# Transfers over 125 and 127 partitions divided at partition 112, a bias added by VectorE, and V's small products spread over more steps of a graph layer

## The chip, the core and the metric

The kernel runs on one core of a Trainium2 chip. A core has five engines with queues of their own: TensorE (PE, with its weight loads shown as PEld), VectorE (DVE), ScalarE (ACT), GpSimd (POOL) and SyncE (SP). Transfers between memory and the on-chip buffers are issued from the queues of SP, ACT and POOL and run on the core's 16 DMA engines. The metric is the device time of one execution in microseconds, lower is better. Times of before: 1989.81, 2000.09 and 2001.78 us, median 2000.09.

## What is computed

One graph layer with a residual. 6250 nodes have 128 features each; 206250 edges are sorted by their target. The features are normalised and clipped at zero, each edge makes a message of its two ends, each node takes the maximum of its messages.

```python
h = jnp.maximum(_layernorm(x, axis=-1), 0.0)
x_i = h[dst]; x_j = h[src]
msg = jnp.concatenate([x_i, x_j - x_i], axis=-1) @ W.T + b
out = jax.ops.segment_max(msg, dst, num_segments=x.shape[0])
return x + jnp.where(jnp.isfinite(out), out, 0.0)
```

Since the target's part of a message is the same for all its edges, the kernel computes A (target part with the bias) and B (source part) for every node once. The result is x + A + the maximum of B over a node's sources.

## The kernel before

All engines' orders are written out by hand: each engine runs its instructions in the order in which the program emits them, and waits only for what it needs. There are four stages.

**Normalisation (to about 278 us).** The 6250 nodes are 50 blocks of L = 125 nodes, a node on each partition; ten blocks (GQ) are loaded as one tile `xs`, partitions 0 to 63 from SP's queue and 64 to 124 from ACT's. Three such tiles are loaded at the start and two more in the loop. `moments` computes mean and variance of ten blocks on VectorE. Then pairs of blocks go round: ACT scales (`xn`), TensorE transposes (`pt`), ACT clips (`hT`), TensorE makes `pm` (for each block a product of ones with `brow`, which holds the bias in its second half, and a product of `hT` with the weights), ACT copies the B half twice (`Bp`, in bf16, and `bo`) and the A half once (`ao`), VectorE and ACT make the two remainders of B in bf16. After ten blocks `bo` and `ao` are stored to the tables `Bt` (SP) and `At` (ACT). From the second ten blocks on, one piece of VectorE work on the edge lists (`pop`) stands behind each pair; a piece `shift` also has TensorE products `dup`.

**Edge lists (278 to 430 us).** VectorE finishes the edge lists; GpSimd begins to gather rows of `Bt` into `G` (each gather is one indirect transfer of 128 rows).

**Loop (430 to 1589 us).** 13 tiles of ten target lanes (49 columns each), 25 steps to a tile; each step handles two blocks. For the step that follows, TensorE makes `z` from V, ACT makes of it the one-hot matrix `oh` in two instructions (`far`, `oh`); for this step TensorE multiplies it with the three bf16 parts of B into `ps` (six products of 490 columns) and VectorE takes the maximum into `acc2`. V of the next tile is prepared beside that: `v_pieces` makes a list of pieces (comparisons and products on VectorE, then `mats`, one for each of the ten lanes, 13 small products on TensorE into `pv`, then ACT's copy to `Vb`), and every step starts with `per` of them, which is two. VectorE also runs through the gathered rows one by one (`stream_step`), and each eight rows go to the table M from SP.

**Tail (from 1589 us).** Five groups of the 49 columns (9, 9, 9, 11 and 11). For each, `xo` (rows of x) is loaded from SP's queue and `a` (rows of A) from ACT's, GpSimd gathers R from M column by column, TensorE transposes a column of `acc` and VectorE merges it with R; then VectorE closes the group with five operations and the result is stored from SP. In the first three groups all 128 lanes have nodes, in the last two the last lane has none. There, and for the first 127 lanes of the others, the transfers have 127 partitions; the 128th lane of the first three groups goes by a transfer of its own.

Of the kernel before, what the change touches and what calls it, by code (L numbers as in the profile page):

```python
# [30 lines left out]
F32 = mybir.dt.float32  # L31
# [8 lines left out]
P = 128  # L40
# [6 lines left out]
L = 125  # L47
LD = 49
# [13 lines left out]
def gnn_kernel(tc, x, src, dst, W, b, out):  # L62
    nc = tc.nc
    N, C = x.shape
# [7 lines left out]
    NBLK = W2 // P  # L72
# [5 lines left out]
    LASTD = N - (P - 1) * LD  # L78
    V = nc.vector
# [11 lines left out]
    with ExitStack() as ctx:  # L91
# [9 lines left out]
        with ExitStack() as body:  # L101
# [52 lines left out]
            with ExitStack() as pre:  # L154
# [13 lines left out]
                brow = pool.tile([1, 2 * C], F32, name="brow")  # L168
                V.memset(brow[:, :C], 0.0)
                nc.sync.dma_start(brow[:, C:], at(b, 0, [[C, 1], [1, C]]))  # L170
# [8 lines left out]
                def load_x(q0):  # L179
                    t = xg[q0] = xp.tile([L, GQ, C], F32, name="xs")  # L180
                    for e, (p0, p1) in zip((nc.sync, A_), ((0, 64), (64, L))):
                        e.dma_start(t[p0:p1], x_q[p0:p1, q0:q0 + GQ])  # L182
# [136 lines left out]
                for q0 in range(0, Q, GQ):  # L319
# [6 lines left out]
                    for i in range(0, GQ, 2):  # L326
# [10 lines left out]
                        for j in range(2):  # L337
                            T_.matmul(pm[:L, j], ones[:1, :L], brow, start=True, stop=False)  # L338
                            T_.matmul(pm[:L, j], hT[:, j, :L], wT, start=False, stop=True)  # L339
                        A_.copy(Bp[:L, 0, q:q + 2], pm[:L, :, :C])  # L340
                        A_.copy(bo[:, i:i + 2], pm[:L, :, :C])  # L341
                        A_.copy(ao[:, i:i + 2], pm[:L, :, C:])
# [6 lines left out]
                    for e, o, t in ((nc.sync, Bt_q, bo), (A_, At_q, ao)):  # L349
                        e.dma_start(o[:, q0:q0 + GQ], t)  # L350
# [73 lines left out]
            with ExitStack() as main:  # L424
# [12 lines left out]
                def v_pieces(t):  # L437
# [23 lines left out]
                    def mats(l):  # L461
                        for b_ in range(NBLK):
# [11 lines left out]
                    for l in range(nl):  # L474
                        ps.append(lambda l=l: mats(l))
# [91 lines left out]
                for d0, g in ((0, cut), (cut, cut), (2 * cut, LASTD - 2 * cut), (LASTD, 11), (LASTD + 11, LD - LASTD - 11)):  # L567
# [3 lines left out]
                    xo = fin.tile([P, GF, C], F32, name="xo")[:np_, :g]  # L571
                    for e, t, s in ((nc.sync, xo, x), (A_, a, At)):
                        e.dma_start(t[:P - 1], at(s, d0 * C, [[LD * C, P - 1], [1, g * C]]))
                        if np_ == P:
                            e.dma_start(t[P - 1:], at(s, ((P - 1) * LD + d0) * C, [[LD * C, 1], [1, g * C]]))
# [16 lines left out]
                    nc.sync.dma_start(at(out, d0 * C, [[LD * C, P - 1], [1, g * C]]), xo[:P - 1])  # L592
                    if np_ == P:
                        A_.dma_start(at(out, ((P - 1) * LD + d0) * C, [[LD * C, 1], [1, g * C]]), xo[P - 1:])
# [62 lines left out]
```

## Time and profile before

| What | Value |
|---|---|
| Median of 3 runs | 2000.09 us |
| The profiled execution, own time | 1993.71 us |
| Its span on the core | 1991.9 us |
| TensorE busy | 1151.7 us, 58% |
| VectorE busy | 954.9 us, 48% |
| ScalarE busy | 767.5 us, 39% |
| GpSimd busy | 724.3 us, 36% |
| Mean granted TensorE clock | 0.764 of 2.4 GHz |
| Moved by DMA | 105.38 MB, mean 53 GB/s |

The busy shares are averages over four stages that are limited by different things, so they are read stage by stage: a table of stretches gives, for each, the busy time of every engine, the granted clock and the DMA share. Within a stage the timeline shows instructions in order of time, with the idle time ahead of each and what ended it. A queue's rows (SPq, ACTq) are issues of transfers; their length is the time that the queue was held by the issue, not the transfer's.

### The profile page before, as it was taken

How to read it: one execution, taken by the hardware profiler on the slowest of the kernel's cores; microseconds unless marked ns; L12 is line 12 of the kernel's file. 1: busy time of each engine (PE TensorE's matmuls, PEld its weight loads, DVE VectorE, ACT ScalarE, POOL GpSimd, SP SyncE). 2: the span in 40 equal slices, each digit the busy share in tenths (PEclk: the TensorE clock that was granted, in tenths of full speed). 3: DMA queues.
4: the chain of work that ended last, by engine and by line, in shares of the span. 5: the costliest groups of instructions: out<-in, count | busy, mean ns of one | idle time of the engine just before them, and what ended most of it. 6: DMA issues, size and time to landing. Idle time of an engine off the chain costs nothing.

```text
span 1991.9 us, 14462 instructions
## 1 busy us (share of the span) xinstructions
PE 1151.7 (58%) x4855; PEld 519.8 (26%) x4862; DVE 954.9 (48%) x1913; ACT 767.5 (39%) x958; POOL 724.3 (36%) x678
## 2 busy tenths in 40 slices
PE   0556677058686878587878778787879800000000
PEld 0222233034242433242433334242424300000000
DVE  4122149865657474947474756656566610110020
ACT  0223212224789454445455554646456800000000
POOL 6000018605646564446455546456551021202000
PEclk9999999557889787787778788768688955555555
DMA  3111011002222222122222222222221011101000
GB/s 79 34 42 32 26 30 36 24 7 65 73 64 81 68 83 66 56 67 70 65 77 70 66 74 75 74 64 71 65 78 52 26 44 36 37 25 38 27 26 23
DMA packets 53775, 105.38 MB, mean 53 GB/s; under 512 B 12342, under 2 KB 31221, under 8 KB 53695
## 3 DMA queue, kind: packets, MB, share of 16 engines
q0 software_dynamic: 21392, 45.22, 8.6%
q1 hardware_dynamic: 21931, 51.21, 7.0%
q10 hardware_dynamic: 10372, 7.98, 1.3%
q8 instruction: 39, 0.64, 0.1%
q14 instruction: 41, 0.34, 0.1%
HBM read 54.91 MB, written 49.45 MB: 52 GB/s over the span
## 4 chain that ended last, share of the span: by engine, by line
PE 35%; another core or an unknown queue 17%; DVE 15%; ACT 12%; issue 9%; POOL 4%; DMA 3%; ACTq 3%; DVEq 0%; POOLq 0%
PE ps L511 14%; PE pv L464 7%; PE z L488 6%; ACT oh L492 5%; ACT far L491 4%; POOL G L88 4%; DVE acc L516 3%; PE pm L339 3%; PE pm L338 3%; DVE G L148 3%; ACTq L182 3%; DMA a<-At 2%; ACT dump L528 1%; DVE OHQ L454 1%
## 5 line engine op out<-in xcount | busy, mean ns | idle before, releaser
L511 PE MATMUL ps<-oh,Bp 126*128 126x490 bf16 (+1 forms) x1950 | 563.9, 427 | 218.0 <-ACT oh L492 88.8
L88 POOL DMA_INDIRECT G<-Bt,ridx x480 | 485.4, 1011 | 416.2 <-DVE G L148 220.3
L516 DVE TENSOR_TENSOR acc<-acc,ps 128x490 f32<-128x490 f32 (+1 forms) x624 | 406.7, 654 | 439.2 <-PE ps L511 267.9
L491 ACT ACTIVATE far<-z 126x980 bf16<-126x980 f32 (+1 forms) x325 | 314.9, 969 | 467.4 <-PE z L488 230.8
L511 PEld LDWEIGHTS <-Bp 126*128 126x128 bf16 x1950 | 193.0, 106 | 558.8 <-issue 364.5
L492 ACT ACTIVATE oh<-far 126x980 bf16<-126x980 bf16 (+1 forms) x325 | 327.5, 1008 | 10.6
L88 POOL DMA_INDIRECT G<-Bt,swin x128 | 161.5, 1262 | 393.9 <-DMA Bt<-bo 247.2
L488 PE MATMUL z<-Vb,Sel 51*126 51x490 bf16 (+1 forms) x650 | 233.1, 444 | 0.7 <-ACT Vb L476 0.7
L464 PE MATMUL pv<-OHD,OHQ 128*50 128x49 bf16 x1664 | 170.1, 276 | 82.2 <-issue 61.3
L148 DVE SCALAR_TENSOR_TENSOR G<-G,slim 128x128 f32<-128x128 f32 x607 | 209.8, 346 | 0.0
L581 PE MATMUL pf<-ident,acc 128*128 128x128 f32 x49 | 20.1, 469 | 300.2 <-DVE R L582 295.7
L464 PEld LDWEIGHTS <-OHQ 128*50 128x50 bf16 x1664 | 161.0, 190 | 121.6 <-issue 95.5
L88 POOL DMA_INDIRECT R<-M,last_e x49 | 47.5, 969 | 257.6 <-DVE R L582 155.5
L488 PEld LDWEIGHTS <-Sel 51*126 51x126 bf16 x650 | 68.1, 147 | 128.7 <-issue 124.0
L344 DVE TENSOR_TENSOR r<-bo,Bp 125x256 f32<-125x256 f32 x25 | 10.6, 426 | 170.2 <-ACT bo L341 170.2
L581 PEld LDWEIGHTS pf<-ident,acc 128*128 128x128 f32 x49 | 8.9, 206 | 311.2 <-DVE R L582 304.5
L588 DVE TENSOR_TENSOR R<-R,a 128x1152 f32<-128x1152 f32 (+1 forms) x5 | 7.3, 1465 | 170.9 <-DMA a<-At 170.8
L297 PE MATMUL dup<-eq,identb 128*128 128x512 bf16 (+1 forms) x245 | 60.8, 371 | 34.6 <-DVE eq L294 27.2
L590 DVE TENSOR_TENSOR R<-R,xo 128x1152 f32<-128x1152 f32 (+1 forms) x5 | 7.3, 1465 | 119.9 <-DMA xo<-in_x 119.9
L333 PE MATMUL pt<-ident,xn 125*128 125x125 f32 x50 | 19.5, 452 | 75.4 <-ACT xn L331 75.4
L339 PE MATMUL pm<-wT,hT 128*125 128x256 f32 x100 | 60.8, 710 | 0.0
L338 PE MATMUL pm<-brow,ones 1*125 1x256 f32 x100 | 60.6, 706 | 0.0
(145 smaller groups left out, 689.8 us busy)
## 6 DMA issues: line engine op xcount, KB each, us to landing
M<-G SPq DMA_DIRECT2D x76, 512.0 KB
G<-Bt,ridx POOLq DMA_INDIRECT x480
Bt<-bo SPq DMA_DIRECT2D x5, 625.0 KB
At<-ao ACTq DMA_DIRECT2D x5, 625.0 KB
G<-Bt,swin POOLq DMA_INDIRECT x128
a<-At ACTq DMA_DIRECT2D x3, 571.5 KB
xo<-in_x SPq DMA_DIRECT2D x3, 571.5 KB
out_x<-xo SPq DMA_DIRECT2D x3, 571.5 KB
```

The source lines that it names most:

```text
L88: G_.indirect_dma_start(out=o, out_offset=None, in_=table, in_offset=bass.IndirectOffsetOnAxis(ap=idx, axis=0))
L148: V.scalar_tensor_tensor(G[:, j], state["prev"], slim[:, k:k + 1], G[:, j], op0=ALU.min, op1=ALU.max)
L182: e.dma_start(t[p0:p1], x_q[p0:p1, q0:q0 + GQ])
L297: T_.matmul(dup[:, c0:c1], identb, e[:, c0:c1], start=s == 1, stop=s == SH)
L338: T_.matmul(pm[:L, j], ones[:1, :L], brow, start=True, stop=False)
L339: T_.matmul(pm[:L, j], hT[:, j, :L], wT, start=False, stop=True)
L464: T_.matmul(st["v"][:, l * LD:(l + 1) * LD], st["q"][:, :Q, c], st["d"][:, :, c], start=b_ == 0, stop=b_ == NBLK - 1)
L488: T_.matmul(z[:, j, :n], Sel[:, i + j], Vb[t % 2][:, :n], start=True, stop=True)
L491: A_.activation(far[:, :, :n], z[:, :, :n], AF.Abs)
L492: A_.activation(oh[:, :, :n], far[:, :, :n], AF.Relu, scale=-1.0, bias=1.0)
L511: T_.matmul(ps[:, :n], Bp[:, e, i + j], oh[:, j, :n], start=e == 0, stop=e == 2)
L516: V.tensor_tensor(a, a, ps[:, :n], ALU.max)
```

## The change

It has three parts.

- Transfers are divided by partition. Over 125 nodes (loads of `xs`, stores of `bo` and `ao`): partitions 0 to 111 and 112 to 124. For `xs` the first part goes from SP, the second from ACT; for a store both parts go from the same queue. In the tail, the three groups with all lanes use one transfer over 128 partitions for each of x, A and the result, and the last two groups use partitions 0 to 111 and 112 to 126; the second part of their store goes from ACT.
- The product of ones with `brow` is gone. The bias is loaded into all 125 partitions (`b_sb`), and VectorE writes `ao` as the sum of the A half of `pm` and the bias, in place of ACT's copy.
- In `v_pieces` a lane's 13 small products are two pieces, of 7 and 6. As every step takes two pieces, they stand in ten steps of a tile and not in five, and the copy to `Vb` stands five steps later.

```diff
+    SPLIT = ((0, L // 16 * 16), (L // 16 * 16, L))
...
-                brow = pool.tile([1, 2 * C], F32, name="brow")
-                V.memset(brow[:, :C], 0.0)
-                nc.sync.dma_start(brow[:, C:], at(b, 0, [[C, 1], [1, C]]))
+                b_sb = pool.tile([L, 1, C], F32, name="b_sb")
+                A_.dma_start(b_sb[:, 0], at(b, 0, [[0, L], [1, C]]))
...
-                    for e, (p0, p1) in zip((nc.sync, A_), ((0, 64), (64, L))):
+                    for e, (p0, p1) in zip((nc.sync, A_), SPLIT):
...
-                            T_.matmul(pm[:L, j], ones[:1, :L], brow, start=True, stop=False)
-                            T_.matmul(pm[:L, j], hT[:, j, :L], wT, start=False, stop=True)
+                            T_.matmul(pm[:L, j], hT[:, j, :L], wT, start=True, stop=True)
...
-                        A_.copy(ao[:, i:i + 2], pm[:L, :, C:])
+                        V.tensor_add(ao[:, i:i + 2], pm[:L, :, C:], b_sb.to_broadcast([L, 2, C]))
...
-                        e.dma_start(o[:, q0:q0 + GQ], t)
+                        for p0, p1 in SPLIT:
+                            e.dma_start(o[p0:p1, q0:q0 + GQ], t[p0:p1])
...
-                    def mats(l):
-                        for b_ in range(NBLK):
+                    def mats(l, r):
+                        for b_ in r:
...
-                        ps.append(lambda l=l: mats(l))
+                        for r in (range(0, 7), range(7, NBLK)):
+                            ps.append(lambda l=l, r=r: mats(l, r))
...
+                    lanes = ((0, P),) if np_ == P else ((0, P - 16), (P - 16, P - 1))
                     for e, t, s in ((nc.sync, xo, x), (A_, a, At)):
-                        e.dma_start(t[:P - 1], at(s, d0 * C, [[LD * C, P - 1], [1, g * C]]))
-                        if np_ == P:
-                            e.dma_start(t[P - 1:], at(s, ((P - 1) * LD + d0) * C, [[LD * C, 1], [1, g * C]]))
+                        for p0, p1 in lanes:
+                            e.dma_start(t[p0:p1], at(s, (p0 * LD + d0) * C, [[LD * C, p1 - p0], [1, g * C]]))
...
-                    nc.sync.dma_start(at(out, d0 * C, [[LD * C, P - 1], [1, g * C]]), xo[:P - 1])
-                    if np_ == P:
-                        A_.dma_start(at(out, ((P - 1) * LD + d0) * C, [[LD * C, 1], [1, g * C]]), xo[P - 1:])
+                    for e, (p0, p1) in zip((nc.sync, A_), lanes):
+                        e.dma_start(at(out, (p0 * LD + d0) * C, [[LD * C, p1 - p0], [1, g * C]]), xo[p0:p1])
```

On TensorE, a pair of blocks in the normalisation stage stood like this before (transposes of the pair, then for each block the bias product and the product with the weights):

```order
L333 MATMUL pt<-ident,xn 128x125 x2
L338 MATMUL pm<-brow,ones 125x256
L339 MATMUL pm<-wT,hT 125x256
L338 MATMUL pm<-brow,ones 125x256
L339 MATMUL pm<-wT,hT 125x256
```

and now like this; the next pair's transposes follow at once:

```order
L333 MATMUL pt<-ident,xn 128x125 x2
L338 MATMUL pm<-wT,hT 125x256 x2
```

On ACT, the head of the program before and now, up to the first scaled block. The loads of `xs` have 13 partitions in place of 61, and the load of the bias stands ahead of them:

```order
L165 DMA lasts_i<-in_dst 1x375x1
L182 DMA xs<-in_x 61x10x128 x3
L251 ACT_TABLE_LOAD
L251 COPY wT<-pm 128x256
L314 ACT_TABLE_LOAD
L314 ACTIVATE rstd<-mv,eps 125x10 x2
```

```order
L166 DMA lasts_i<-in_dst 1x375x1
L170 DMA b_sb<-in_L_gnn_b 125x128
L182 DMA xs<-in_x 13x10x128 x3
L251 ACT_TABLE_LOAD
L251 COPY wT<-pm 128x256
L314 ACT_TABLE_LOAD
L314 ACTIVATE rstd<-mv,eps 125x10 x2
```

On SP, the last two groups of the tail, from the third group's store on. A group's load of x stands behind the store of the group ahead of it in both orders; before, one transfer of 127 partitions each:

```order
L592 DMA out_x<-xo 127x1152
L573 DMA xo<-in_x 127x1408
L592 DMA out_x<-xo 127x1408
L573 DMA xo<-in_x 127x1408
L592 DMA out_x<-xo 127x1408
```

and now two loads and, for SP, the larger part of each store:

```order
L594 DMA out_x<-xo 128x1152
L576 DMA xo<-in_x 112x1408
L576 DMA xo<-in_x 15x1408
L594 DMA out_x<-xo 112x1408
L576 DMA xo<-in_x 112x1408
L576 DMA xo<-in_x 15x1408
L594 DMA out_x<-xo 112x1408
```

## Rows read from the trace of the kernel before

**Rows 1.** Stretches: length, busy us (instructions) by engine, granted clock, DMA share, GB/s.

```profile
278.20:430.00 151.80, 66.21 (x381) 36.98 (x386) 124.07 (x130) 22.84 (x14) 80.79 (x48) 0.70 0.11 30
430.00:1589.50 1159.50, 918.79 (x4144) 410.56 (x4143) 712.41 (x1510) 678.31 (x763) 566.14 (x560) 0.81 0.21 67
1589.50:1991.90 402.40, 20.07 (x49) 8.89 (x49) 50.23 (x76) 0.00 (x0) 47.49 (x49) 0.50 0.09 32
```

**Rows 2.** Stretches again: stores of 125 partitions, a 127-partition transfer, a write of M.

```profile
282.00:290.00 8.00, 7.38 (x30) 3.07 (x29) 7.17 (x8) 0.00 (x0) 0.00 (x0) 1.00 0.35 103
1870.00:1895.00 25.00, 0.00 (x0) 0.00 (x0) 0.00 (x0) 0.00 (x0) 0.00 (x0) 0.50 0.06 27
908.20:909.60 1.40, 1.40 (x5) 0.51 (x4) 0.44 (x1) 1.37 (x2) 0.00 (x0) 0.50 0.93 374
```

**Rows 3.** Timeline of the tail: start, length, engine, line, operation, [idle before <-releaser].

```profile
1605.86 0.97 DVE L587 TENSOR_SCALAR none<-R 128x1152 f32<-128x1152 f32 x1
...
1637.26 1.36 DVE L588 TENSOR_TENSOR R<-R,a 128x1152 f32<-128x1152 f32 x1 [30.42 <-DMA a<-At]
...
1642.76 0.33 DVE L582 SCALAR_TENSOR_TENSOR R<-R,limp,pf 128x128 f32<-128x128 f32 x1
...
1643.22 19.25 SPq L573 DMA_DIRECT2D xo<-in_x  x1
...
1644.39 0.94 POOL L88 DMA_INDIRECT R<-M,last_e  x1 [0.30 <-issue]
...
1649.24 0.76 DVE L587 TENSOR_SCALAR none<-R 128x1152 f32<-128x1152 f32 x1
...
1960.38 0.23 SPq L592 DMA_DIRECT2D out_x<-xo  x1
```

**Rows 4.** Timeline of one pair's products in the normalisation; then the page's group r.

```profile
106.20 1.21 PE L338 MATMUL pm<-brow,ones 1*125 1x256 f32 x2
106.31 0.38 ACT L335 ACTIVATE hT<-pt 128x250 f32<-128x250 f32 x1 [0.56 <-PE pt L333]
...
107.34 1.22 PE L339 MATMUL pm<-wT,hT 128*125 128x256 f32 x2
...
L344 DVE TENSOR_TENSOR r<-bo,Bp 125x256 f32<-125x256 f32 x25 | 10.6, 426 | 170.2 <-ACT bo L341 170.2
```

**Rows 5.** Timeline of the start; then, from the waits, ACT's waits on its issues.

```profile
2.31 40.90 ACTq L182 DMA_DIRECT2D xs<-in_x  x3
...
34.58 0.75 DVE L312 BATCH_NORM_AGGREGATE mv<-stats 125x2 f32<-125x6 f32 x10
...
49.83 0.48 ACT L331 ACTIVATE xn<-xs,nmr,rstd 125x128 f32<-125x128 f32 x1
...
ACT xn L331 <- issue: 12.7, 2, 6.8
```

**Rows 6.** Timeline of the loop, ninth tile, steps 10 to 20: ACT's far, TensorE's products.

```profile
1212.74 0.99 ACT L491 ACTIVATE far<-z 126x980 bf16<-126x980 f32 x1 [0.92 <-PE z L488]
...
1217.13 2.67 PE L464 MATMUL pv<-OHD,OHQ 128*50 128x49 bf16 x26 [1.81 <-DVE OHQ L454]
...
1220.74 2.63 PE L511 MATMUL ps<-oh,Bp 126*128 126x490 bf16 x6
...
1221.30 0.99 ACT L491 ACTIVATE far<-z 126x980 bf16<-126x980 f32 x1 [6.53 <-PE z L488]
...
1226.45 1.42 PE L511 MATMUL ps<-oh,Bp 126*128 126x490 bf16 x6
...
1245.44 0.99 ACT L491 ACTIVATE far<-z 126x980 bf16<-126x980 f32 x1 [6.47 <-PE z L488]
...
1257.09 0.99 ACT L491 ACTIVATE far<-z 126x980 bf16<-126x980 f32 x1
```

## The prediction

> **What bounds the kernel now.** I read the stage table first (busy time by stretch). It cuts the span in a loop of 1159.5 us in which TensorE is busy for 918.79 us at a mean granted clock of 0.81 of 2.4 GHz, a stretch before it in which VectorE is busy for 124.07 of 151.8 us, and a tail of 402.4 us in which no engine is busy for more than 50.23 us [rows 1]. The 278.2 us ahead of these are the normalisation stage. So the tail is bound by something that is no engine. The DMA rates say what: while a transfer of 127 partitions is alone in flight, the core's 16 DMA engines are 0.06 busy, one sixteenth, and move 27 GB/s; while two stores of 125 partitions run, the share is 0.35 and the rate 103 GB/s; during one write of M, 128 partitions, it is 0.93 and 374 GB/s [rows 2]. The partition count sets how many engines work. The tail's timeline shows the price: VectorE waits 30.42 us for a group's rows of A and x, works 5.50 us (1637.26 to 1642.76), and the cycle starts again [rows 3]. In the normalisation stage ACT, TensorE and VectorE hand one pair of blocks round in series [rows 4], and ACT's own issue of x loads stops it [rows 5]. In the loop a pair's step takes about 2.3 us without V products and up to 8.6 us with them [rows 6].
>
> **The tail.** Edit: three groups load, and store, 128 partitions in one transfer; the last two go as 112 and 15. By rows 2 that takes 571.5 KB from about 22 us to under 2. What is left is VectorE's own chain, in the order it has today. Nine columns of R take 6.48 us (1642.76 to 1649.24), 0.72 each. The closing operations of such a group take 0.77 for the first and 5.50 for the other four, 6.27, or 0.70 a column. For 49 columns: 49 x 1.42 = 69.6 us. The first group is paced by its gathers: its closing begins at 1605.86, 16.4 us after the tail's start instead of 6.5, so 9.9 more. The last store: today 31.5 us pass from its issue at 1960.38 to the end of the span; 698.5 KB at 27 GB/s are 25.9 of them, so 5.6 are fixed, and at 374 GB/s it is 1.9 + 5.6 = 7.5. Sum 87 us against 402.4: **-315 us**. Three things are taken as hidden. GpSimd's gathers cost 0.95 + 0.30 each, 61 us for 49, under the 69.6. The next group's x load still stands behind this group's store on SP (1643.22, just after the copy of 1637.26 to 1642.76 ended), so it has 6.48 + 0.77 us and two of the four closing operations, some 10 us, as cover; store and load together are 1.14 MB, 3.1 us at 374 GB/s, plus the fixed 5.6, near 9. If that cover is missed by 5 us in each of five groups, the gain is 290. Past the best case, with the first group's 9.9 also gone, it is 325. In the last two groups ACT's load of A now stands behind ACT's 15-partition store, thus behind VectorE's closing too; it has the same cover. One issue more or less a group on SP and ACT is off the path, since neither queue has anything else to do there. A part of 15 partitions is in no row. Between one engine (82.5 KB at 27 GB/s, 3.1 us) and many (under 0.3) the last store differs by 3 us at most, the other parts lie under the cover; I take many, as the 0.35 for 125 shows that it need not be one.
>
> [...]
>
> **Normalisation, TensorE.** Each of 50 blocks loses its bias product. In a pair the first one starts at 106.20 and holds the product with hT until 107.34, though hT is ready at 106.31 + 0.38 = 106.69: 0.6 us. The second stands in the chain with its whole 1.14 us (the spacing of 106.20 and 107.34). So 1.74 x 25 = **-43.5 us**. The pair is one serial loop, so nothing else steps in its place. VectorE's new addition writes 125x256; its nearest row is r of the same shape, 426 ns, before which VectorE idles 170.2 us in 25 pairs, 6.8 each, for ACT's bo. The addition can run while ACT makes Bp and bo, so I cost it at nothing; were it to stand ahead of r it would cost 25 x 0.43 = 11 us. ACT's dropped copy of ao ran while ACT waited for r anyway: nothing.
>
> **Normalisation, loads.** ACT issues three x loads of 61 partitions and is held until 2.31 + 40.90 = 43.21 us, though the statistics it needs next stand at 34.58 + 0.75 = 35.33; its first xn comes at 49.83 [rows 5]. With 13 partitions it has a fifth of the rows, on many engines. I take 9 us: 7.9 from those two times and a little for the work that then also falls ahead of 35.33 (bounds 5 to 13). Twice later ACT's xn waits on its own issue, 12.7 us in all [rows 5]; I take 12 of it (bounds 6 to 12.7). The bias row, loaded to 125 partitions, is 62.5 KB on ACT's queue, which no longer blocks. SP's loads grow from 64 to 112 partitions, but SP has nothing else to do. The store of Bt in front of the first gathers gets faster as well; that I cost at nothing, since the stretch behind it is VectorE's (124.07 us busy of 151.8) and the gathers run beside that. Two issues per store in place of one: SP idles, and ACT pays five issues more, which I leave to the bounds. Dropping brow's memset and load saves nothing, as VectorE's next work there waits for a load of dst. **-21 us**.
>
> **The loop.** V's products for the next tile stand in steps 10 to 14 of 25, 26 to a step; they will stand in steps 10 to 19, 13 to a step. The work is the same; what can change is how they mix. From step 10 at 1212.74, five steps with products take 32.70 us, the next five without take 11.65, 44.35 together [rows 6]. 26 products take 2.67 us, so 13 take 1.33. Added to a plain step of 2.33 that is 3.66, ten steps 36.6: -7.7 a tile, x 12 tiles with products = -93. That needs TensorE at its upper level, where six products of ps take 1.42. At its lower level they take 2.63, 1.21 more, so 4.87 a step and 48.7 for ten: +4.4 a tile, +52. Which one? After 26 products the ps products behind them run at 2.63 (1220.74), yet one step on at 1.42 (1226.45) [rows 6], so the level recovers between groups even today, and smaller groups leave a larger share to the big products. I take eight steps at the upper level and two at the lower: 39.0, -5.3 a tile, **-64 us**. Nothing waits for the later end: V is copied at step 20, and step 24 is the first to read it.
>
> **Sum.** 315 + 43.5 + 21 + 64 = 443.5. The profiled execution took 1993.7 us (span 1991.9 and 1.8 around it): **1550 us**. The median of the three runs is 2000.1, 6 above it, which is within their spread.
>
> **Rivals.** (1) The loop loses: the spread products hold TensorE at 1.2 GHz through ten steps instead of five, +52 instead of -64. For it: 2.63 at 1220.74. Time 1993.7 - 379.5 + 52 = 1666. (2) The loop gains all: 1993.7 - 379.5 - 93 = 1521, and lower where the waits behind the products shrink with them; for it speaks that five steps cost 32.70 us and their products only 5 x 2.67 = 13.4. (3) The split brings nothing, because two parts share what one had; only the product and the loop count: 1993.7 - 43.5 - 64 = 1886. Against it stand the rates of rows 2. [...] (4) Slower: a step's price comes from changing between small and large products, not from their number. The first product step takes 1212.74 to 1221.30, 8.56 us; if all ten cost that, a tile loses 85.6 - 44.35 = 41.2, twelve 495, against 379.5 gained: 2109. It decides from 379.5 / 120 = 3.2 us above today's mean of 4.44, that is 7.6 us a step; the mean of the five product steps today, 6.54, is below that, and gives 1866.
>
> **How the numbers follow.** The forecast, with the loop between -105 and -20, 0.55; rival 1, with anything from there to +80, 0.22; rival 2, 0.18; rival 3, 0.03; rival 4, 0.02. The tail's bounds add -10 to +25, the small terms -4 to +20. The forecast's own range is 1500 to 1620. To leave out no more than 2 in 10, I take rival 2 down to 1455 and rival 1 up to 1670. A measurement of this kernel tells about 1% from no change. Faster by over 1% holds everything but rival 4: 0.97; slower 0.02, and 0.01 for sums that cancel.
>
> **What would show it.** Right: a tail of 80 to 110 us with VectorE busy for half or more of it and no wait for A or x over 3 us; a pair of blocks 1.7 us shorter than now; the first xn before 43 us; a tile of the loop in 80 to 90 us. Wrong: waits for xo of 5 us and more in the tail (the cover misses), ps products at 2.63 through steps 10 to 19, or a tile above 93 us.

## The result and the profile after

The changed kernel took 1595.55 us (median of 4 runs, 1586.28 to 1602.89), the kernel before 1994.95 us beside it (4 runs, 1969.96 to 2001.78). The ratio is 0.806 with a 95% interval of 0.795 to 0.816; it leaves out the two runs of before that are more than 1.5% slower than its fastest, and so lies above the quotient of the medians, 0.80. The profiled execution took 1599.15 us, its span 1597.4. Forecast were 1550 us, 1455 to 1670.

The stage table of the changed kernel (as [rows 1]: stretch, length, busy us and instructions of PE, PEld, DVE, ACT and POOL, granted clock, DMA share, GB/s); its four stages are the normalisation from its first xn on, the edge list, the loop and the tail:

```profile
42.20:218.30 176.10, 81.44 (x180) 42.28 (x183) 53.77 (x163) 56.15 (x153) 3.48 (x1) 0.90 0.15 37
218.30:370.00 151.70, 66.24 (x381) 36.85 (x385) 123.84 (x131) 22.59 (x13) 76.57 (x48) 0.68 0.11 30
370.00:1492.30 1122.30, 902.08 (x4139) 409.97 (x4138) 710.39 (x1507) 679.46 (x763) 565.27 (x560) 0.84 0.22 69
1492.30:1597.40 105.10, 21.04 (x57) 9.25 (x54) 51.70 (x79) 0.00 (x0) 49.68 (x49) 0.51 0.41 123
```

Against [rows 1] the normalisation ends at 218.3 in place of 278.2 (-59.9), the edge list is unchanged (151.7 against 151.8), the loop has 1122.3 in place of 1159.5 (-37.2) and the tail 105.1 in place of 402.4 (-297.3). Together these are 394.5 us, the difference of the two profiled executions.

Stretches of the changed kernel's tail in which the 128-partition loads run, against the 127-partition ones of [rows 2], and one with the last group's loads and a store in flight:

```profile
1497.50:1499.00 1.50, 0.00 (x0) 0.00 (x0) 0.00 (x0) 0.00 (x0) 1.02 (x2) 0.50 1.01 412
1577.00:1578.00 1.00, 0.49 (x1) 0.20 (x1) 0.41 (x2) 0.00 (x0) 0.00 (x0) 0.50 0.98 220
```

By these shares all 16 engines work: 0.06 and 27 GB/s became 1.01 and 412. In the second row the engines are as busy, 0.98, but move 220 GB/s.

VectorE's timeline in the tail (start, length, engine, line, operation, [idle before <- releaser]), with one of TensorE's transposes and SP's last store:

```profile
1508.57 0.76 DVE L588 TENSOR_SCALAR none<-R 128x1152 f32<-128x1152 f32 x1
...
1521.92 0.76 DVE L588 TENSOR_SCALAR none<-R 128x1152 f32<-128x1152 f32 x1
...
1534.83 0.76 DVE L588 TENSOR_SCALAR none<-R 128x1152 f32<-128x1152 f32 x1
...
1545.69 0.35 DVE L583 SCALAR_TENSOR_TENSOR R<-R,limp,pf 128x128 f32<-128x128 f32 x1 [1.43 <-remote]
...
1548.90 0.49 PE L582 MATMUL pf<-ident,acc 128*128 128x128 f32 x1 [2.32 <-issue]
...
1551.29 0.35 DVE L583 SCALAR_TENSOR_TENSOR R<-R,limp,pf 128x128 f32<-128x128 f32 x1 [2.44 <-remote]
...
1562.17 0.89 DVE L588 TENSOR_SCALAR none<-R 127x1408 f32<-127x1408 f32 x1
...
1578.03 0.89 DVE L588 TENSOR_SCALAR none<-R 127x1408 f32<-127x1408 f32 x1
1581.43 1.63 DVE L589 TENSOR_TENSOR R<-R,a 127x1408 f32<-127x1408 f32 x1 [2.50 <-DMA a<-At]
...
1588.15 0.33 SPq L594 DMA_DIRECT2D out_x<-xo  x1
```

The wait of 30.42 us in [rows 3] is gone; one of 2.50 is left. From one closing to the next pass 13.35, 12.91, 27.34 and 15.86 us. The third of these holds the columns of group 4, which come every 2.8 us behind a wait for "remote", a releaser that the profile can't name.

One pair of the normalisation, as [rows 4], on ACT and VectorE, with TensorE's products for the next:

```profile
51.86 0.37 ACT L339 CAST Bp<-pm 125x256 bf16<-125x256 f32 x1 [2.16 <-PE pm L338]
52.13 0.38 ACT L340 COPY bo<-pm 125x256 f32<-125x256 f32 x1
52.54 0.42 DVE L341 TENSOR_TENSOR ao<-pm,b_sb 125x256 f32<-125x256 f32 x1 [4.10 <-ACT bo L340]
52.88 0.42 DVE L343 TENSOR_TENSOR r<-bo,Bp 125x256 f32<-125x256 f32 x1
...
55.08 0.38 ACT L335 ACTIVATE hT<-pt 128x250 f32<-128x250 f32 x1 [0.56 <-PE pt L333]
...
55.52 2.07 PE L338 MATMUL pm<-wT,hT 128*125 128x256 f32 x4 [0.47 <-ACT hT L335]
57.62 0.37 ACT L339 CAST Bp<-pm 125x256 bf16<-125x256 f32 x1 [2.16 <-PE pm L338]
```

A pair takes 57.62 - 51.86 = 5.76 us. But the addition stands ahead of r after all: it starts at 52.54, just after ACT has read the same PSUM tile for bo (52.13 + 0.38 = 52.51), and r starts 0.34 us behind it.

### The profile page after: what moved, and what is told of

It is laid out like the page before. It is cut to its first block, busy times and chain, and to the rows that moved or that the text cites. A ratio compares the mean times of both kernels' runs of the same rounds, so it can differ in the third digit from the quotient of the medians.

```text
span 1597.4 us, 14322 instructions
## 1 busy us (share of the span) xinstructions
PE 1073.3 (67%) x4756; PEld 499.2 (31%) x4762; DVE 963.3 (60%) x1937; ACT 761.7 (48%) x933; POOL 721.4 (45%) x678
## 4 chain that ended last, share of the span: by engine, by line
PE 40%; DVE 14%; ACT 12%; issue 12%; POOL 5%; another core or an unknown queue 4%; DMA 1%; ACTq 0%; DVEq 0%; SPq 0%; POOLq 0%
PE ps L512 20%; PE pv L464 10%; PE z L489 8%; ACT far L492 5%; ACT oh L493 5%; POOL G L89 5%; DVE acc L517 3%; DVE G L149 3%; DVE OHQ L454 1%; ACT dump L529 1%; DVE OHD L454 1%; DVE OHD L459 1%; DVE big L549 1%; PE pf L582 1%
## 5 line engine op out<-in xcount | busy, mean ns | idle before, releaser
L512 PE MATMUL ps<-oh,Bp 126*128 126x490 bf16 (+1 forms) x1950 | 545.1, 417 | 199.3 <-ACT oh L493 98.7
L464 PE MATMUL pv<-OHD,OHQ 128*50 128x49 bf16 x1664 | 183.3, 277 | 79.4 <-issue 64.4
L489 PE MATMUL z<-Vb,Sel 51*126 51x490 bf16 (+1 forms) x650 | 227.4, 434 | 2.8 <-issue 2.0
L464 PEld LDWEIGHTS <-OHQ 128*50 128x50 bf16 x1664 | 165.2, 189 | 142.9 <-issue 122.9
L341 DVE TENSOR_TENSOR ao<-pm,b_sb 125x256 f32<-125x256 f32 x25 | 10.6, 425 | 109.7 <-ACT bo L340 104.3
L454 DVE TENSOR_TENSOR OHD<-TD,IQ 128x910 bf16<-128x910 bf16 (+1 forms) x91 | 52.9, 619 | 12.8 <-PE pv L464 12.7
L338 PE MATMUL pm<-wT,hT 128*125 128x256 f32 x100 | 51.4, 667 | 11.8 <-ACT hT L335 11.8
L459 DVE TENSOR_TENSOR OHD<-OHD,TV 128x910 bf16<-128x910 bf16 (+1 forms) x91 | 52.8, 619 | 0.0
L454 DVE TENSOR_TENSOR OHQ<-TQ,IQ 128x1300 bf16<-128x1300 bf16 (+1 forms) x65 | 50.9, 818 | 0.0
L297 PEld LDWEIGHTS <-identb 128*128 128x128 bf16 x252 | 26.1, 104 | 73.5 <-issue 54.2
```

The costliest lines, as they stand in the source:

```text
L297: T_.matmul(dup[:, c0:c1], identb, e[:, c0:c1], start=s == 1, stop=s == SH)
L338: T_.matmul(pm[:L, j], hT[:, j, :L], wT, start=True, stop=True)
L454: V.tensor_tensor(st[key][:, a:b_, :m], mid_bcast(src_[:, s], b_ - a), IQ[:, a + off:b_ + off, :m], ALU.is_equal)
L459: V.tensor_tensor(o, o, mid_bcast(TV[:, s], b_ - a), ALU.mult)
L464: T_.matmul(st["v"][:, l * LD:(l + 1) * LD], st["q"][:, :Q, c], st["d"][:, :, c], start=b_ == 0, stop=b_ == NBLK - 1)
L489: T_.matmul(z[:, j, :n], Sel[:, i + j], Vb[t % 2][:, :n], start=True, stop=True)
```

## The experiments

Where a stage is named, its length is from the stage table of that run; a table of the loop's steps stands behind the experiments on the loop.

**1. The tail alone.** The kernel before with this part of the change:

```
-  e.dma_start(t[:P - 1], ...)            (127 partitions, then 1)
+  lanes = ((0, P),) if np_ == P else ((0, P - 16), (P - 16, P - 1))
+  for p0, p1 in lanes: e.dma_start(t[p0:p1], ...)
```

> The kernel before with the tail's part of the change alone (128-partition transfers in three groups, 112 and 15 partitions in two). Theory: the tail is its own stage and depends on nothing else of the change: it falls from 402.4 to about 105 us as in the changed kernel, the rest stays, so about 1995 - 297 = 1698 us. Rival: part of the tail's gain comes with the other parts (M's last writes and the gathers arriving earlier in the shorter loop): then the tail stays above 120 us and the time above 1712 us.

Measured: 1684.12 us (1676.30 to 1686.22) beside 1999.51, ratio 0.8425 (0.8385 to 0.8464).

```profile
430.10:1580.60 1150.50, 928.67 (x4140) 412.84 (x4140) 710.55 (x1507) 678.48 (x763) 563.40 (x560) 0.80 0.21 67
1580.60:1682.80 102.20, 20.99 (x56) 9.24 (x54) 52.13 (x79) 0.00 (x0) 49.61 (x49) 0.52 0.43 126
```

The tail falls by 300.2 us with nothing else changed, so its gain is its own. The whole is 14 us below the theory's figure: 3 of that in the tail, 9 in the loop, which was not touched (1150.5 against 1159.5): the loop differs from run to run, by up to 30 us in the changed kernel (1102.9 to 1132.7, listed under 7).

**2. V's products back in five steps,** in the changed kernel:

```
-  for r in (range(0, 7), range(7, NBLK)):
+  for r in (range(0, NBLK),):
```

> The changed kernel with V's products back in five steps of 26. Theory: the loop's shortening (1159.5 to 1122.3 us) comes from the spread products alone, so the loop returns to 1150 to 1165 us and the whole to about 1595 + 37 = 1632 us. Rival: the late signals in the loop move with whatever comes ahead of it, and the spread itself is worth little: then the loop stays below 1140 us and the whole below 1615 us. What the prediction said (64 us) would give 1659 us.

Measured: 1634.14 us (1627.27 to 1641.28), ratio 0.8173 (0.8133 to 0.8213).

```profile
369.30:1532.60 1163.30, 928.53 (x4138) 412.41 (x4138) 710.57 (x1507) 678.34 (x763) 568.45 (x560) 0.79 0.21 66
```

The loop is 41.0 us longer than the changed kernel's 1122.3, and 35 longer than the mean of experiments 3 and 4 (1124.7 and 1132.7), which ran on the same chip with the changed loop. The theory holds in size: the spread products are worth 35 to 41 us, not 64.

**3. The normalisation's transfers as before** (x in 64 and 61 partitions, stores of 125 in one):

```
-  zip((nc.sync, A_), SPLIT)
+  zip((nc.sync, A_), ((0, 64), (64, L)))
-  for p0, p1 in SPLIT: e.dma_start(o[p0:p1, ...], t[p0:p1])
+  e.dma_start(o[:, ...], t)
```

> The changed kernel with the normalisation's transfers as before: x loads of 64 and 61 partitions, stores of 125 in one. Theory, from the two traces: the first xn returns from 42.15 to about 50 us (+8), ACT's issue waits at the later loads return (+5), and the last store of Bt, ahead of the first gathers, takes about 13 us again in place of 5 (+8 if something waits for it): the stretch ahead of the loop grows from 370 by 13 to 21 us, the whole to about 1595 + 17 = 1612 us. Rival: the loads' faster landing is hidden but for ACT's own issue, +5 us or less, 1600 us.

Measured: 1613.83 us (1609.04 to 1619.33), ratio 0.809 (0.805 to 0.813). The loop begins at 387.8 in place of 370.0: +17.8, inside the theory's 13 to 21; the first xn stands at 52.30 in place of 42.15.

**4. The bias as a product again,** with ACT's copy of ao:

```
+  T_.matmul(pm[:L, j], ones[:1, :L], brow, start=True, stop=False)
-  V.tensor_add(ao[:, i:i + 2], pm[:L, :, C:], b_sb.to_broadcast([L, 2, C]))
+  A_.copy(ao[:, i:i + 2], pm[:L, :, C:])
```

> The changed kernel with the bias again as a product into pm, and ACT's copy of ao. Theory: a pair of blocks returns from 5.75 to 7.46 us, 25 x 1.71 = 43 us, and the whole comes to 1638 us. Rival: the two products would overlap with the faster loads' slack, and VectorE's addition, which stands in front of r for 0.34 us a pair, has eaten part of the gain: then it costs under 30 us and the whole is under 1625 us.

Measured: 1629.45 us (1624.12 to 1643.35), ratio 0.814 (0.811 to 0.817). The loop begins at 411.8, +41.8 us, and two successive Bp of ACT stand at 47.65 and 55.10, 7.45 apart; from the pair's hT to its Bp pass 4.57 us, in the changed kernel 2.54 (55.08 to 57.62), and so in the median of its 25 pairs:

```profile
47.65 0.37 ACT L341 CAST Bp<-pm 125x256 bf16<-125x256 f32 x1 [4.19 <-PE pm L340]
...
50.53 0.38 ACT L336 ACTIVATE hT<-pt 128x250 f32<-128x250 f32 x1 [0.56 <-PE pt L334]
...
55.10 0.37 ACT L341 CAST Bp<-pm 125x256 bf16<-125x256 f32 x1 [4.19 <-PE pm L340]
```

The theory holds in the trace. The profiled execution took 1643.35 us, 44 more than the changed kernel's: 41.8 here, 10 more in the loop, 8 less in the tail (taken up under 5). The median lies only 34 us above; what made the other five executions shorter no trace shows. Parts 3 and 4 make 17.8 + 41.8 = 59.6 of the 59.9 us: the normalisation is accounted for.

**5. The tail's transposes ahead of the columns:**

```
   for j in range(j0, min(j0 + 4, g)):
       T_.transpose(p[:, j - j0], acc_v[:, d0 + j], ident)
+  for j in range(j0, min(j0 + 4, g)):
       V.scalar_tensor_tensor(R[:, j], R[:, j], limp[...], p[:, j - j0], ...)
```

> The changed kernel with the tail's four transposes of a PSUM tile in front of the four columns of R that read it, rather than one transpose before each. Theory: the changed kernel's columns take 0.93 us and not the 0.72 of the prediction because each transpose waits for VectorE's read of the same tile; ahead of them, 0.72, so the tail falls from 105 by about 49 x 0.21 = 10 us to 95 us. Rival: the columns are paced by GpSimd's gathers, one every 1.25 us: then nothing changes, 100 to 105 us.

Measured: one run of 1570.02 us. The tail has 94.9 us, which looks like the theory. But experiments 3, 4, 6, 7, 9 and 10, whose tails are the changed kernel's word for word, have 95.1 to 97.1, and 1, 2, 8 and 11, with the same tail, 101.8 to 106.9. VectorE's timeline tells what the edit does:

```profile
1537.67 1.88 DVE L584 SCALAR_TENSOR_TENSOR R<-R,limp,pf 128x128 f32<-128x128 f32 x7
1545.06 0.35 DVE L584 SCALAR_TENSOR_TENSOR R<-R,limp,pf 128x128 f32<-128x128 f32 x1 [5.50 <-DMA R<-M,last_e]
1549.77 0.35 DVE L584 SCALAR_TENSOR_TENSOR R<-R,limp,pf 128x128 f32<-128x128 f32 x1 [4.36 <-DMA R<-M,last_e]
```

Seven columns run through in 1.88 us, and then VectorE waits 5.50 and 4.36 us for gathered rows. The rival holds: behind the transposes GpSimd's gathers are next, and the edit is worth a microsecond or two at most. The premise was wrong as well: in groups 2 and 3 the changed kernel's cycles of 13.35 and 12.91 us less 6.4 for the closing leave 0.77 and 0.72 a column. The 8 to 10 us by which its tail exceeds 95 to 97 come with group 4's late columns: their cycle took 27.34 us against 16.3 in experiment 6, the next one 15.86 against 19.8 there (columns waiting for gathered rows), and the last group then waits 2.50 us for A, which 6 does not. The late columns stood in experiments 1, 2, 8 and 11 too (tails of 102.2, 106.9, 105.2 and 101.8), and not in 6 and 7, with 95.9 and 95.1.

**6. The addition behind r:**

```
-  V.tensor_add(ao[:, i:i + 2], pm[:L, :, C:], ...)
   r1 = lw.tile([L, 2, C], F32, name="r1")
   V.tensor_tensor(r1, bo[:, i:i + 2], Bp[:L, 0, q:q + 2], ALU.subtract)
+  V.tensor_add(ao[:, i:i + 2], pm[:L, :, C:], ...)
```

> The changed kernel with VectorE's addition of the bias written behind the first subtraction r instead of in front of it. Theory: the addition starts only when ACT has read the same PSUM tile for bo, so it holds r up by 0.34 us; behind r it stands beside ACT's copy, a pair becomes about 0.3 us shorter, and the loop's first far comes about 8 us earlier than 372.6. Rival: the addition is hidden where it stands, as the prediction had it: within 2 us.

Measured: one run of 1570.44 us; the loop begins at 362.5 in place of 370.0, 7.5 us earlier.

```profile
47.54 0.42 DVE L342 TENSOR_TENSOR r<-bo,Bp 125x256 f32<-125x256 f32 x1 [4.10 <-ACT bo L340]
47.88 0.42 DVE L343 TENSOR_TENSOR ao<-pm,b_sb 125x256 f32<-125x256 f32 x1
...
52.97 0.42 DVE L342 TENSOR_TENSOR r<-bo,Bp 125x256 f32<-125x256 f32 x1 [4.11 <-ACT bo L340]
```

A pair takes 52.97 - 47.54 = 5.43 us, 0.33 less, and the addition runs beside ACT's copy. The theory holds: where it stood, the addition was on the path, and 25 times 0.33 come to the 7.5 us and a little.

**What the loop's steps show.** The change's ten steps with products did not get shorter (43.7 us a tile before, 44.1 after; table below), and the gain stood in steps 20 to 24 (19.0 to 13.3), where the only change is that ACT's copy to Vb now stands in step 20. So something moved between the steps that is not tied to the work in them. The changed kernel's timeline, tile 0, shows it (PE, ACT, DVE and POOL):

```profile
420.34 0.62 PE L489 MATMUL z<-Vb,Sel 51*126 51x490 bf16 x2
...
421.14 0.99 ACT L492 ACTIVATE far<-z 126x980 bf16<-126x980 f32 x1 [1.38 <-PE z L489]
...
423.62 0.62 PE L489 MATMUL z<-Vb,Sel 51*126 51x490 bf16 x2
...
425.62 0.94 POOL L89 DMA_INDIRECT G<-Bt,swin  x1 [0.31 <-issue]
...
426.90 0.62 PE L489 MATMUL z<-Vb,Sel 51*126 51x490 bf16 x2
...
428.39 0.99 ACT L492 ACTIVATE far<-z 126x980 bf16<-126x980 f32 x1 [5.20 <-PE z L489]
428.44 0.67 DVE L517 TENSOR_TENSOR acc<-acc,ps 128x490 f32<-128x490 f32 x1 [3.51 <-PE z L489]
...
430.33 0.97 ACT L492 ACTIVATE far<-z 126x980 bf16<-126x980 f32 x1
```

By its records TensorE goes on at its pace: z at 420.34, 423.62 and 426.90, 3.28 us apart. ACT takes the first one at 421.14. The second, finished at 424.24 by its record, it takes at 428.39, 4.1 us late; VectorE is released at the same moment, and the third z's far follows directly. The trace also records updates of semaphores; those of TensorE's are called its signals here. They agree with the late starts: no signal of TensorE arrives from 423.98 to 428.37, then four in 0.25 us. Just before, GpSimd ends a run of eight gathers (the last issue begins at 425.62), and its last rows have landed 0.45 us before the signals come. In the loops of both kernels there are 16 places each where TensorE's signals stop for 3.5 to 15.8 us and then come three or more within 0.45 us; in 22 of the 32 the release stands 0.38 to 0.78 us behind a gather's landing, where under a fifth of all instants of the loops lie in such a stretch. These are called held signals below; whether the signal or the product behind it was late is left open.

The pages' shares of the chain that ended last have a line for releasers that the profile can't name, "another core or an unknown queue". Here it is for the kernel before, for experiment 1 and for the changed kernel:

```profile
PE 35%; another core or an unknown queue 17%; DVE 15%; ACT 12%; issue 9%; POOL 4%; DMA 3%; ACTq 3%; DVEq 0%; POOLq 0%
```

```profile
PE 42%; DVE 18%; ACT 14%; issue 11%; POOL 5%; ACTq 3%; another core or an unknown queue 3%; DMA 2%; DVEq 0%; POOLq 0%
```

```profile
PE 40%; DVE 14%; ACT 12%; issue 12%; POOL 5%; another core or an unknown queue 4%; DMA 1%; ACTq 0%; DVEq 0%; SPq 0%; POOLq 0%
```

The 17% are not the held signals alone. The chain of the kernel before in order of time (start, length) puts most of them into the tail:

```profile
1650.00 45.53 another core or an unknown queue
...
1801.90 48.90 another core or an unknown queue
1854.18 43.21 another core or an unknown queue
```

Seven such pieces, 259.5 of 342 us, are waits of the tail, and experiment 1 took them away without touching the loop. The other 82.5 us stand in the loop; in the changed kernel, of 69 us, 66 do.

**7. The loop without gathers:** one plain load of eight rows a partition on SP's queue in place of eight gathers on GpSimd's.

```
-  gather(G[:, j], Bt[:, :], idx)                 (8 of them)
+  nc.sync.dma_start(G, Bt[:1024].rearrange("(p u) c -> p u c", u=U))
```

> The changed kernel with the loop's 608 gathers left out: each group of eight is read by one plain load of 512 KB of fixed rows of Bt on SP's queue, so M holds other values and out is another; GpSimd does nothing in the loop. Theory: the steps of 4 to 11 us that stand where the work in them is 1.9 to 3.3 us come with GpSimd's gathers. Then they go: a tile takes 72 to 78 us in place of about 90, and the loop falls from 1118 to 980 to 1020 us; V's products in ten steps take 36 to 40 us. Rival: they belong to TensorE's own instruction stream or to its clock: then the loop stays above 1080 us.

Measured: 1431.58 us (two runs), ratio 0.719 (0.716 to 0.722).

```profile
368.90:1333.40 964.50, 833.61 (x4139) 393.88 (x4138) 704.26 (x1507) 678.69 (x763) 0.00 (x0) 0.93 0.22 80
```

The changed kernel's loop without an edit in it took 1122.3, 1124.7, 1132.7, 1102.9 and 1110.3 us (its own run, 3, 4, 5, 6). The last two ran on the same chip as this one: against them the loop falls by 142 us to 964.5, against the changed kernel's own run by 158, with M's writes of 512 KB and all the work of TensorE, ACT and VectorE still there. (Of the 608 gathers left out, 48 stood ahead of the loop.) No place is left where signals stop and then come in a bunch (nor in 9), the chain has no share of an unknown releaser any more, and tiles 8 to 10 take 74.9 us each, alike step by step. The granted clock is 0.93 in place of 0.84; how much of these us is time at TensorE's lower level, and whether the waits bring it, is not shown. The theory holds, with more gained than it expected.

**8. z ahead of V's pieces** in a step of the loop, with all gathers:

```
-  for f in pend[:per]: f()
-  pend = pend[per:]
   nxt = z_and_onehot(*pairs[k + 1]) if k + 1 < len(pairs) else None
+  for f in pend[:per]: f()
+  pend = pend[per:]
```

> The changed kernel with a step's z products written ahead of the same step's pieces of V (V's products and VectorE's comparisons), so that TensorE hands z to ACT before it takes up the 13 products. Theory: with products, a step is a chain through ACT: z waits behind 1.33 us of products, far and oh behind z. Then ten steps lose up to 10 us a tile and the loop up to 100 us (to 1020 to 1080 us). Rival: TensorE's own work or the late steps beside the gathers pace it, and the order inside a step changes less than 20 us (loop 1098 to 1135 us).

Measured: 1578.91 us (1574.15 to 1585.45), ratio 0.793 (0.790 to 0.797), the loop 1100.6 us. Against 5 and 6 on the same chip (1102.9 and 1110.3) that is 6 us less than their mean, no more than these two differ. The rival holds. The ten steps with products do shrink (44.1 us in the changed kernel to 39.3), but steps 20 to 24 take more for it (13.3 to 15.0), and steps 0 to 9 too (32.4 to 33.5): beside the gathers what one step gives, others take back.

**9. The loop without gathers and with V's products in five steps** (the edits of 2 and 7 together):

> As the run with plain loads in place of the gathers (out again another), but with V's products in five steps of 26. It gives the price of the split alone, without the signals that the gathers hold back. Theory: the forecast's arithmetic was right for TensorE itself (39.0 against 44.35 us for steps 10 to 19; 38.4 were measured without gathers), so these ten steps take 42 to 45 us here, steps 20 to 24 stay at 10.5, and the loop is 40 to 70 us longer than 960. Rival: of the 44.35 us, some were signals held back, and the products in five steps cost little more than in ten: ten steps of 38 to 41 us, the loop within 30 us of 960; what the split gains beside the gathers then lies in where the held signals fall.

Measured: one run of 1472.13 us.

```profile
369.90:1374.90 1005.00, 868.16 (x4140) 399.92 (x4139) 706.60 (x1507) 679.28 (x763) 0.00 (x0) 0.86 0.21 77
```

The loop is 40.5 us longer than in 7, which ran on another chip; steps 10 to 19 take 42.0 us a tile in place of 38.4, at the lower edge of the theory's 42 to 45, steps 20 to 24 as much as there. So the split alone is worth 3.6 us a tile. In total that is the size of experiment 2 again, where it lay in other steps; and the gathers cost the five-step order 158 us (1163.3 to 1005.0), the ten-step order 142 to 158.

**10. One gather a column,** written between the columns instead of eight at once:

```
-  gather_group()                    (allocates G, issues 8)
+  gather_group(0)                   (allocates G, queues 8)
+  gather_some(1)                    (issues one, at every column)
```

> The changed kernel with the loop's gathers issued one a column instead of eight at once; the same gathers, buffers and bytes. Theory: TensorE's signals arrive late while GpSimd issues one gather behind another (in the changed kernel they come in bunches about 0.45 us after a gather's landing, 1.8 us after the last of a burst); with a pause after each gather no signal is held for long, the steps of 5 to 11 us go, and the loop falls from 1118 to 980 to 1040 us. Rival: each gather holds the signals for its own time, however the gathers stand: then the loop stays within 30 us of 1118.

Measured: 1579.07 us (1567.24 to 1606.24), ratio 0.792 (0.786 to 0.799), the loop 1105.2 us, among the unedited ones. That would speak for the rival, had the edit done what it says. GpSimd's timeline:

```profile
604.78 0.94 POOL L89 DMA_INDIRECT G<-Bt,ridx  x1 [6.21 <-DVE G L157]
...
613.52 0.94 POOL L89 DMA_INDIRECT G<-Bt,ridx  x1 [0.30 <-issue]
621.45 0.95 POOL L89 DMA_INDIRECT G<-Bt,ridx  x1 [6.99 <-DMA M<-G]
```

Eight still follow one another at 1.25 us (604.78 to 613.52): nothing on GpSimd waits for a column, only for a buffer. The run tells nothing on the theory.

**11. Groups of two gathers in 24 buffers,** so that a buffer, and with it GpSimd's wait, comes every two:

```
-  U = 8          GB = 6
+  U = 2          GB = 24
```

> The changed kernel with groups of two gathers in 24 buffers in place of groups of eight in 6 (same bytes, same look-ahead; M written 128 KB at a time, 304 times). Each buffer comes free with its own write of M, so GpSimd now really stops after two gathers. Theory: TensorE's signals are held for as long as gathers follow one another; bursts of 2.5 us in place of 10 us and more leave no step above about 2 us late: the loop falls from 1118 to 980 to 1060 us. Rival: each of the 560 gathers holds the signals for its own time however they stand: the loop stays at 1090 to 1140 us.

Measured: 1488.50 us (1480.10 to 1497.19) beside 1984.72, ratio 0.749 (0.744 to 0.755). The loop, and GpSimd in it:

```profile
369.70:1393.70 1024.00, 859.61 (x4139) 400.59 (x4139) 707.82 (x1507) 679.62 (x763) 577.50 (x560) 0.89 0.26 76
```

```profile
1000.34 0.94 POOL L89 DMA_INDIRECT G<-Bt,ridx  x1 [1.07 <-DVE G L149]
1001.59 0.94 POOL L89 DMA_INDIRECT G<-Bt,ridx  x1 [0.30 <-issue]
1003.62 0.94 POOL L89 DMA_INDIRECT G<-Bt,ridx  x1 [1.09 <-DVE G L149]
...
1018.89 0.94 POOL L89 DMA_INDIRECT G<-Bt,ridx  x1 [0.30 <-issue]
```

GpSimd is as busy as before (577.5 us, 565.3 in the changed kernel) with the same gathers, and the loop is 98 us shorter than the changed kernel's and 79 shorter than the shortest of the unedited ones (1102.9); five places with held signals are left, where the runs with groups of eight have 8 to 16. The theory holds in the loop's length: how the gathers stand decides, at the same number of them. It was not clean in one point: where GpSimd had fallen behind, longer runs still stand (1012.56 to 1018.89 has six), and steps 0 to 9 still take 31.1 us against 27.0 without gathers. The edit also divides M's writes; that these matter by themselves isn't excluded, but with 512 KB writes and no gathers (7) nothing was held. This version is faster than both kernels: its interval, 0.744 to 0.755, lies below the changed kernel's, 0.795 to 0.816.

The loop's steps in these runs: mean us over the first 12 tiles, worked out from the starts of ACT's far.

```
                                    steps 0-9  10-19  20-24   loop (stage)  clock
before                                29.9      43.7   19.0     1159.5      0.81
2  products in five steps             29.8      44.5   18.9     1163.3      0.79
changed kernel                        32.4      44.1   13.3     1122.3      0.84
8  z ahead of V's pieces              33.5      39.3   15.0     1100.6      0.84
10 one gather a column                32.0      42.9   13.4     1105.2      0.86
11 groups of two                      31.1      38.7   11.7     1024.0      0.89
9  no gathers, five steps             27.1      42.0   10.8     1005.0      0.86
7  no gathers, ten steps              27.0      38.4   11.1      964.5      0.93
12 four edits                         27.2      36.6   12.1      955.9      0.93
```

**12. Four edits together** (5, 6, 8 and 11):

> The run with groups of two gathers, and with it the three other edits: transposes ahead in the tail, the addition behind r, and z ahead of V's pieces in a step. Theory: the four act in different places and add up: the tail and the normalisation give about 8 us each, z first about 20 us as it did beside groups of eight, 1488.5 - 36 = 1452 us, and more where no held signal hides what z first gives (its first step with products, 6.9 us, became 3.2: up to 44 us, 1428 us). Rival: with the signals no longer held, TensorE's own work is the limit and z first gives nothing: 1472 us.

Measured: 1414.54 us (1413.49 to 1415.84), but beside 1844.82 us for the kernel before (1836.98 to 1851.33), ratio 0.7675 (0.7645 to 0.7706). On this chip the kernel before is some 145 us faster than in all other comparisons, so the 1414.54 can't be set beside 1452 or 1428, and the ratio not beside 0.749. Neither theory nor rival is decided. The trace shows no place with held signals, a loop of 955.9 us (table), and a tail of 94.7; z first gives 38.4 to 36.6 us in ten steps and costs 1.0 in the five behind them, against experiment 7. That this chip holds signals back less than the others would explain the faster kernel before, its 145 us being near the 142 to 158 of experiment 7; no trace of that kernel on that chip shows it, and it stays open.

## Why the prediction came out as it did

**The size and the sign** were right: -394.5 us by the profiled executions, -443.5 forecast, within the range. The signs that were named came out for the tail (105.1 us, no wait for A or x over 2.50, VectorE busy for 49% where half was named), for the pair (7.46 to 5.76 us) and for the first xn (42.15). The 49 us that were missing lie in the tail (18), the loop (27) and the normalisation (4.6). Rivals 1, 2 and 4 fall with the loop's -37 (they needed +52, -93 and +495), rival 3 with the tail's -297.

**The tail** (-315 forecast, -297.3 measured, -300.2 alone). Cause and most terms held: the first closing 16.3 us into the tail (16.4 forecast), two of the cycles 13.35 and 12.91 us for 9 x 1.42 = 12.8, one of 15.86 for 11 x 1.42 = 15.6. The step that failed is "49 x 1.42" as the only thing on the path. The cycle of group 4 took 27.34 us where the columns of 11 and the closing of 9 make 11 x 0.72 + 9 x 0.70 = 14.2: 13 us, the late columns of experiment 5. They are late signals like those of the loop, though not in bunches, with GpSimd issuing one gather behind the other: the transpose recorded from 1548.90 to 1549.39 releases VectorE at 1551.29, 1.9 us later, where one of group 3, ending at 1532.15, did so at 1532.19; the gathered row that the same column needs had landed at 1542.13 by the semaphore events. That the gathers cause it in the tail too was not tested there. Nor are the gathers hidden where no signal is held: in experiments 5 and 6 the last columns wait for their rows. The last group's wait for A (2.50) is the cover that the prediction put at some 10 us for near 9: its price of store and load went by 374 GB/s, and at 1577.00, three transfers of some 700 KB in flight, the rate is 220. The last store took 9.25 us (1588.15 to 1597.40) for the 7.5. No row shows a transfer of 112 partitions: the 374 GB/s for it was an estimate from the 128 of [rows 2]. From 1589.0 to 1592.0, with this store's parts of 112 and 15 in flight, the rate is 230 GB/s at a DMA share of 0.78.

**The bias product** (-43.5 forecast, 41.8 measured). "I cost it at nothing" was wrong: the addition waits for ACT's read of bo, stands ahead of r, and costs 7.5 us (experiment 6), within the 11 that the prediction named for that case. The products gave more than the 43.5: from hT to Bp a pair takes 2.03 us less (4.57 to 2.54), 51 us in 25 pairs, not 1.74. The prediction took out the two bias products and left the two others their 1.14 us each and 0.12 behind them, 2.40; without bias products between them they take 2.10 (55.52 to 57.62). That the term came out within 2 us is luck: two errors of some 7 us cancel.

**The loads** (-21 forecast, 17.8 measured). The first xn came 7.7 us earlier (49.83 to 42.15) for the 9 forecast, and ACT's waits on its own issue fell from 12.7 to 5.3 us where 12 were to go. The three loads at the start hold ACT's queue for 4.83 us in place of 40.90. That 13 partitions go on many engines stood in no row; by the packets in the trace the third of these loads moves its 65 KB from 11.71 to 13.53 us, up to 8 packets at a time, where those of 61 partitions had 2 at most and, alone, 20 GB/s (25 to 40 us). The store of Bt ahead of the first gathers, costed at nothing, brought nothing that shows: the edge list is as long as before.

**The loop** (-64 forecast; -37.2 between the two traces, 35 to 41 by single edits). The step that failed is the base: "44.35 together" for steps 10 to 19 was read from one tile and taken as TensorE's own work at its two levels. (In the trace of the kernel before one product of ps starts 206 ns after the other where the granted clock is 1.0, and 407 ns where it is 0.50, in the median; with 490 columns to a product that is 2.4 and 1.2 columns a ns, which the prediction writes as GHz.) Without gathers the five-step order takes 42.0 us and the ten-step order 38.4, near the 39.0 forecast. So the term was 3.6 us a tile, not 5.3; 12 x 3.6 = 43. The rest of the 44.35 goes with the gathers, which neither order removes: two of the 16 places with held signals, ending at 1228.63 and 1245.41, lie in the five product steps of the very tile that was read. That is also why the sign that the prediction named came out mixed: "a tile in 80 to 90 us" holds for the mean (89.7) but for five tiles only; "a tile above 93" came in five, three of them tiles 1, 3 and 4, which carry other work. And the gain appeared in steps 20 to 24, which the prediction took as untouched. The few us between 43 and 35 to 41 are within the loop's spread, while every loop with five product steps beside gathers (1150.5 to 1163.3) lies above every one with ten and the gathers in groups of eight (1100.6 to 1132.7).

What the prediction had no term for is the held signals. Without gathers the loop is 142 to 158 us shorter, some four times what the spread products were worth. The page's line on releasers without a name would have pointed at them only after a look at where in time it stands: of its 17% in the kernel before, three quarters are the tail's waits, which the prediction did take out, and 82.5 us are in the loop.

## What to carry to other kernels

In a tail where no engine is busy and the DMA share stands at one sixteenth, look at the transfer's partition count: here 128 partitions in place of 127, or 112 and 15, took the wait away (30.42 us to 2.50 at most), and VectorE's chain was what was left. Look where in time a share of the chain stands before it is put down to a cause: most of the 17% here was the tail, not the loop. A term that is sized from one tile can hold waits that the edit does not touch; take it from the mean of several tiles, and look for late starts that the work in a step does not explain. An edit that is to space out what an engine issues must give that engine something to wait for; here a different place in the program gave it none, and the gathers still stood 1.25 us apart (experiment 10).

## What was not expected of the hardware

Beside runs of GpSimd's gathers TensorE's signals reached ACT and VectorE up to 15.8 us after the signal before them, in bunches. Taking the gathers out shortened the loop by 142 to 158 us in either order of the products; giving them pauses after two shortened it by 79 to 98 us. The waits are of ACT and VectorE for TensorE's signals. What holds the signals is open, and the records don't tell whether the products themselves or their signals were late.
